# The order of a factorization kernel comes from 24 rounds of its list scheduler, with shorter transfer times in its model

## The chip, the cores and the metric

The kernel runs on one core of a Trainium2 chip. The metric is the device time of one execution in microseconds (us), as the median of several runs; less is better. The core has five instruction queues that run beside each other and meet through semaphores: TensorE (PE, matmuls into the PSUM banks), VectorE (DVE), ScalarE (ACT), GpSimd (POOL) and SyncE (SP, which only issues transfers). GpSimd issues transfers too. Each engine works through its own instructions strictly in the order in which the program was written, so an instruction whose input is late holds everything behind it on its engine.

## The reference

With x of 1024 x 512 and a weight of 64 x 512 x 512 (embedding e, feature f, model column m):

```python
out_lin = x @ lin_w.T + lin_b
xv = jnp.einsum('bf,efm->bem', x, weight)
zp = jnp.einsum('bf,efm->bem', jnp.square(x), jnp.square(weight))
interaction = 0.5 * jnp.sum(jnp.square(xv) - zp, axis=1)
return out_lin + interaction
```

So 64 products of 1024 x 512 by 512 x 512 are squared and summed over e. The second einsum needs only the sum over e of the squared weights, and so one product.

## The kernel before

The columns of the weight are worked off in groups of model columns: two narrow groups of 16 and twenty wide groups of 24, each with all 64 embeddings (`groups`, L41). In a group the product is not formed directly: x and the weight are each split in 2 x 2 blocks, and seven products of block sums replace eight (the loop over `ORDER` at L737, tiles X1 to X7 of x). Each of the seven is split again: six by the same scheme (`tree`, L513, seven products of two matmuls each), and product 1 in a wide group by a scheme of 20 smaller products (`wide_tree`, L598, HK at L20). What saves matmuls costs adds: block sums of the weight are made by GpSimd (the `t` tiles) and by transfers that add into memory (`dma_add`, L342), and the partial products that come out of PSUM are combined by VectorE, ScalarE and GpSimd into the tiles `oa`, `ob` and `c`. A finished block is squared by ScalarE (`square`, L324) and summed over e by VectorE (`reduce`, L328) into `acc`. The squares of the weight (`wsq`) go the same way into `w2_sum`.

PSUM is small: four pairs of banks, `b1`, `b3`, `b2_0` and `b2_1`. A product that accumulates into a bank can't start before VectorE or ScalarE has read what it held. So the reads of the banks (`tt`, L301, and `copy`, L315) release matmuls, and matmuls release reads.

None of this is emitted in the order of the source. Each helper records an operation in a `Plan` (L45) with a modelled duration for each engine that can do it, and with the operations that it depends on. A matmul has a `key`, its place in the intended sequence of TensorE. `Plan.order` (L76) then runs once: it gives every operation a latest start, worked back from the time at which the matmuls that need it would run if TensorE never waited, and plays the program through in modelled time. Whenever an engine is free, `pick` (L127) gives it the ready operation with the smallest latest start; TensorE takes the ready matmul of the smallest key within 20 us of its plan. The sequence in which operations were picked is the program, engine by engine. Only the order survives: the chip keeps no modelled time. Transfers have a modelled duration as well (`dma`, L339; `dma_add`, L342; the weight loads in `load`, L471), during which SyncE counts as taken.

After the last group an epilogue squares x once more (L775 to L783, which overwrites tiles that are free by then), adds the stored `acc` and linear parts (`add_acc`, L789) and multiplies by `w2_sum` (L805 to L826).

Of the kernel before, what the change touches and what calls it, by code (L numbers as in the profile page):

```python
# [32 lines left out]
HLEAD = 0  # L33
TBUF = 3
SPARE = -99.0
AHEAD = 20.0
APART = True
PE, DVE, ACT, POOL, SP = "PE", "DVE", "ACT", "POOL", "SP"
# [6 lines left out]
class Plan:  # L45
# [27 lines left out]
            op.key = op.after = max(key, op.after + 1e-6)  # L73
        self.ops.append(op)

    def order(self, spare=SPARE):  # L76
        ops = self.ops
        chain = sorted((o for o in ops if o.key is not None), key=lambda o: o.key)
        t = 0.0
        for o in chain:  # L80
            o.latest = t
            t += o.costs[PE]
        for o in reversed(ops):
            for d in o.deps:
                ops[d].succ.append(o.n)
            o.waits = [ops[d] for d in o.deps if o.key is None or ops[d].key is None]
        waiting = [len(o.succ) for o in ops]
        stack = [o for o in ops if not o.succ]
        while stack:
            o = stack.pop()  # L90
            latest = t if o.latest is None else o.latest
            cost = min(o.costs.values()) + o.land + self.HOP
            for x in o.succ:
                if o.key is None or ops[x].key is None:
                    latest = min(latest, ops[x].latest - cost)
            o.latest = latest
            for d in o.deps:
                waiting[d] -= 1
                if not waiting[d]:
                    stack.append(ops[d])  # L100
# [26 lines left out]
        def pick(e, now):  # L127
            if e == PE:
                able = [n for n in pending[e]
                        if ops[n].latest < now - late + AHEAD and ready(ops[n]) <= now + 1e-6]  # L130
                return ops[min(able, key=lambda n: ops[n].key)] if able else None
            if APART and e == POOL and free[DVE] > now + 0.1 and running[DVE].both:
                return None
            at = {n: ready(ops[n]) for n in pending[e]}
            for n in sorted((n for n in at if at[n] <= now + 1e-6),
                            key=lambda n: (ops[n].latest, n)):
                o = ops[n]
                if len(o.costs) > 1 and e == DVE and o.latest + late - now > spare:
                    continue
                if APART and o.both and e == DVE and free[POOL] > now + 0.1:  # L140
                    continue
                until = now + o.costs[e]
                if not any(
                    now + 1e-6 < at[u] < until - 0.2
                    and ops[u].latest < o.latest
                    and ops[u].latest + late < until + 0.1
                    for u in at
                ):
                    return o
            return None  # L150

        while len(done) < len(ops):
            now = heapq.heappop(times)
            moved = True
            while moved:
                moved = False
                for e in pending:
# [4 lines left out]
                        continue  # L162
                    moved = True
                    if e == PE:
                        late = max(late, now - o.latest)
                    cost = o.costs[e]

                    if e == DVE and o.both and free[POOL] > now + 0.1:
# [51 lines left out]
def kernel(  # L220
# [121 lines left out]
    def dma_add(o, i, rows, reads, writes):  # L342
        token = ("token", len(plan.ops))

        def emit(_):
            nc.gpsimd.dma_start(o, i, accum_op=ALU.add)

        cost = 2.9 * rows / 1024
        plan.add({POOL: 1.0}, emit, reads + writes, writes + (token,), land=cost + 2.5)
        plan.add({SP: cost}, None, (token,), ())  # L350

# [119 lines left out]
    def load(g, names):  # L471
        iw = GROUPS[g] // 2 * E
        for name, q in names:
            for k in range(KH):
                o = reg(name, k * iw, iw)
                dma(o.ap, source(g, q)[:, k * iw:(k + 1) * iw], (), o.atoms, 2.4 * iw / 1024)

    def outer_sum(g, which):
        o, i = {
# [404 lines left out]
```

## Time and profile before

| | us |
|---|---|
| median of 3 runs | 1427.72 |
| lowest and highest of them | 1426.12 and 1429.38 |
| span of the profiled execution, first to last instruction | 1425.4 |
| TensorE busy in it, matmuls | 1407.8 |
| VectorE busy | 1123.7 |
| ScalarE busy | 731.2 |
| GpSimd busy | 1093.3 |

The profiled execution has a span and no time of its own beside it; the runs that give the median were made without a profile. In the views below a row of instructions in order of time gives the start in us from the span's start, the duration, engine, line, operation, what is written from what (buffer numbers left out), shape and count, and in brackets the engine's idle time before it and what ended it. A product of the kernel is one matmul in the source and two matmul records in the trace. Rows of L356 are products of the two schemes, of L309 adds, of L335 sums over e, of L319 and L318 copies out of PSUM, of L779 and L793 the epilogue.

### The profile page before, as it was taken

To read this page: it belongs to the slowest core of one execution; us is meant where nothing else is said; L and a number is where in the kernel's file an instruction comes from. 1 tells how busy PE (TensorE), PEld (TensorE's weight loads), DVE (VectorE), ACT (ScalarE), POOL (GpSimd) and SP (SyncE) were. 2 spreads that over 40 slices of the span, in tenths; PEclk is the share of its full clock that TensorE was granted. 3 is DMA by queue.
4 is the path that set the end of the run, shared out by engine and by line. 5 is a ranking of instruction groups with operands and counts; after the bars stand their busy time and mean duration, and the time that the engine had idled before them with its cause. 6 is when DMAs were issued, how large, how long until landed. Compare 5 with 4: busy or idle time off the path is not lost.

```text
span 1425.4 us, 14830 instructions
## 1 busy us (share of the span) xinstructions
PE 1407.8 (99%) x4680; PEld 883.2 (62%) x4680; DVE 1123.7 (79%) x1365; ACT 731.2 (51%) x1048; POOL 1093.3 (77%) x895
## 2 busy tenths in 40 slices
PE   8999999999999999999999999999999999999998
PEld 3887565666656566665656566665656666565653
DVE  2678778796977879697887879687787969778875
ACT  2446545463645646464554646465464646455431
POOL 7897869696787869687776968787686968878670
PEclk9999999999999999999999999999999999999999
DMA  7667636464653646465463645555364646545241
GB/s 237 183 142 177 150 84 160 116 142 109 141 130 95 163 89 162 102 138 135 109 155 86 156 118 133 125 125 136 89 166 102 156 104 143 129 99 133 67 131 61
DMA packets 78893, 184.53 MB, mean 129 GB/s; under 512 B 28064, under 2 KB 29088, under 8 KB 78816
## 3 DMA queue, kind: packets, MB, share of 16 engines
q1 hardware_dynamic: 65488, 115.17, 27.5%
q0 software_dynamic: 12752, 67.38, 25.1%
q10 hardware_dynamic: 576, 1.05, 0.2%
q8 instruction: 38, 0.62, 0.2%
q14 instruction: 39, 0.32, 0.1%
HBM read 127.04 MB, written 6.19 MB: 93 GB/s over the span
## 4 chain that ended last, share of the span: by engine, by line
PE 91%; DVE 6%; issue 1%; DMA 1%; POOL 1%; ACT 0%; SPq 0%; DVEq 0%; POOLq 0%
PE b L356 75%; PE b_r L356 6%; PE b_l L356 6%; DVE acc L335 1%; DVE ob L309 1%; PE b_l L393 1%; DVE oa L309 1%; PE b_r L393 1%; PE b_l L813 1%; PE b_r L813 1%; DVE p L309 1%; DVE w_sum L335 1%; DMA X<-xT 1%; DVE c L309 0%; DMA ob<-lin_wT 0%
## 5 line engine op out<-in xcount | busy, mean ns | idle before, releaser
L356 PE MATMUL b<-t,X 128*128 128x384 f32 (+1 forms) x2144 | 720.9, 476 | 5.1 <-DVE oa L309 3.3
L356 PEld LDWEIGHTS b<-t,X 128*128 128x128 f32 x2144 | 403.2, 190 | 266.9 <-issue 23.2
L356 PE MATMUL b<-w,X 128*128 128x384 f32 (+1 forms) x816 | 276.1, 474 | 0.0
L309 POOL TENSOR_TENSOR t<-w 128x768 f32<-128x768 f32 (+1 forms) x128 | 182.4, 1431 | 119.7 <-PE b_l L356 104.4
L326 ACT ACTIVATE oa<-oa 128x768 f32<-128x768 f32 (+1 forms) x176 | 144.6, 824 | 201.6 <-DVE oa L309 182.9
L356 PEld LDWEIGHTS b<-w,X 128*128 128x128 f32 x816 | 154.6, 190 | 98.3 <-ACT p L319 13.0
L319 ACT COPY p<-b 128x768 f32<-128x768 f32 (+1 forms) x158 | 122.3, 774 | 173.4 <-PE b L356 173.2
L335 DVE TENSOR_REDUCE acc<-oa 128x12 f32<-128x768 f32 (+1 forms) x176 | 158.6, 921 | 39.9 <-ACT oa L326 39.8
L335 DVE TENSOR_REDUCE w_sum<-wsq 128x12 f32<-128x768 f32 (+1 forms) x176 | 158.6, 921 | 27.7 <-ACT wsq L326 27.7
L309 POOL TENSOR_TENSOR t<-w,t 128x384 f32<-128x384 f32 (+1 forms) x136 | 141.9, 1043 | 4.9
L319 ACT COPY b<-b 128x768 f32<-128x768 f32 (+1 forms) x134 | 102.5, 765 | 74.7 <-PE b L356 70.1
L309 DVE TENSOR_TENSOR oa<-b,oa 128x768 f32<-128x768 f32 (+1 forms) x66 | 61.3, 929 | 86.1 <-PE b L356 86.1
L326 ACT ACTIVATE wsq<-w 128x768 f32<-128x768 f32 (+1 forms) x132 | 104.9, 823 | 46.8 <-DMA w<-weight 31.8
L309 POOL TENSOR_TENSOR ob<-ob,p 128x768 f32<-128x768 f32 (+1 forms) x44 | 78.8, 1791 | 22.9 <-DVE p L309 22.9
L326 ACT ACTIVATE c<-c 128x768 f32<-128x768 f32 (+1 forms) x88 | 70.4, 819 | 47.9 <-DVE c L309 46.6
L356 PE MATMUL b<-T,X 128*128 128x384 f32 (+1 forms) x264 | 92.3, 476 | 0.0
L309 POOL TENSOR_TENSOR t<-t,w 128x256 f32<-128x256 f32 (+1 forms) x80 | 90.2, 1202 | 0.0
L309 DVE TENSOR_TENSOR ob<-b,oa 128x768 f32<-128x768 f32 (+1 forms) x66 | 61.3, 929 | 30.0 <-PE b L356 30.0
L309 DVE TENSOR_TENSOR p<-b,p 128x768 f32<-128x768 f32 (+1 forms) x88 | 81.5, 926 | 1.1 <-ACT wsq L326 0.6
L326 ACT ACTIVATE ob<-ob 128x768 f32<-128x768 f32 (+1 forms) x88 | 71.0, 826 | 21.6 <-DVE ob L309 14.6
L309 DVE TENSOR_TENSOR oa<-oa,b 128x768 f32<-128x768 f32 (+1 forms) x88 | 81.2, 923 | 0.8
L309 DVE TENSOR_TENSOR ob<-ob,b 128x768 f32<-128x768 f32 (+1 forms) x88 | 80.0, 926 | 2.0 <-PE b L356 1.4
(118 smaller groups left out, 2130.8 us busy)
## 6 DMA issues: line engine op xcount, KB each, us to landing
w<-weight SPq DMA_DIRECT2D x120, 384.0 KB, 3.5
T<-weight SPq DMA_DIRECT2D x40, 384.0 KB, 4.2
w<-T POOLq DMA_DIRECT2D x20, 768.0 KB, 5.8
T1a<-weight SPq DMA_DIRECT2D x20, 384.0 KB, 3.7
w22a<-weight SPq DMA_DIRECT2D x20, 384.0 KB, 3.2
T1a<-weight POOLq DMA_DIRECT2D x10, 768.0 KB, 7.9
T<-T1a POOLq DMA_DIRECT2D x10, 768.0 KB, 7.5
T1b<-weight SPq DMA_DIRECT2D x20, 384.0 KB, 4.5
```

Of the source, the lines that this page charges most:

```text
L309: return f(o.ap, a.ap, b.ap)
L319: return nc.scalar.copy(o.ap, i.ap)
L326: lambda _: nc.scalar.activation(o.ap, i.ap, AF.Square), i.atoms, o.atoms)
L335: nc.vector.tensor_reduce(o, x, axis=AX.X, op=ALU.add)
L356: nc.tensor.matmul(a.ap, b.ap, w.ap, start=start, stop=True, skip_group_check=True)
L393: nc.tensor.matmul(o[j].ap, x.ap[:, ts((g * 2 + j) % (NB // 2), P)], w.ap, start=(k == 0), stop=(k == NK - 1),)
L813: nc.tensor.matmul(z.ap, view(xe[h, k // KH])[:, k % KH, ts((g * 2 + j) % (NB // 2), P)], reg("w2_sum", k * M, M).ap, start=(k == 0), stop ...
```

## The change

`Plan.order` no longer plays the program through once. It calls the former body, now `schedule`, 24 times. After each round `blame` goes through the matmuls in the order of the round. For one that began more than 0.05 us later than TensorE was free, it follows back, up to 12 steps, what the matmul waited for: the slowest input of an operation if that came last, or else the operation before it on its engine. Each operation of that chain gets a `boost`, twice the time lost and at least 0.4 us, which makes its latest start earlier in the following rounds; boosts add up. The round in which the last matmul ends soonest in the model is the program. Matmuls keep their own due times (`due`), which boosts don't move. The modelled duration of a transfer that adds goes from 2.9 to 2.4 us per 1024 columns, and that of a weight load from 2.4 to 2.0.

```diff
+ROUNDS = 24
+CHAIN = 12
+PUSH = 2.0
...
-    def order(self, spare=SPARE):
+    def order(self):
+        boost, best = defaultdict(float), None
+        for o in reversed(self.ops):
+            for d in o.deps:
+                self.ops[d].succ.append(o.n)
+            o.waits = [self.ops[d] for d in o.deps
+                       if o.key is None or self.ops[d].key is None]
+        for _ in range(ROUNDS):
+            done = self.schedule(boost)
+            end = max(o.end for o, e in done if e == PE)
...
+            if best is None or end < best[0]:
+                best = end, done
+            self.blame(done, boost)
+        return best[1]
+
+    def blame(self, done, boost):
+
+        before, last, free = {}, {}, 0.0
+        for o, e in done:
+            before[o.n] = last.get(e)
+            last[e] = o
+            o.engine = e
+
+        def slowest(o):
+            return max((self.ops[d] for d in o.deps), key=lambda d: d.end, default=None)
+
+        for o, e in done:
+            if e != PE:
+                continue
+            lost = o.end - o.costs[PE] - free
+            free = o.end
+            if lost < 0.05:
+                continue
+            x = slowest(o)
+            for _ in range(CHAIN):
+                if x is None or x.engine == PE:
+                    break
+                begin = x.end - x.land - x.costs[x.engine]
+                y = slowest(x)
+                if y is not None and y.end + self.HOP > begin - 0.03:
+                    x = y
+                    continue
+                boost[x.n] += PUSH * max(lost, 0.2)
+                x, y = before[x.n], x
+                if x is None or x.latest > y.latest + 0.5:
+                    break
+
+    def schedule(self, boost, spare=SPARE):
         ops = self.ops
         chain = sorted((o for o in ops if o.key is not None), key=lambda o: o.key)
         t = 0.0
         for o in chain:
-            o.latest = t
+            o.latest = o.due = t
             t += o.costs[PE]
...
-            latest = t if o.latest is None else o.latest
+            latest = t if o.key is None else o.due
...
-            o.latest = latest
+            o.latest = latest - boost[o.n]
...
-                        if ops[n].latest < now - late + AHEAD and ready(ops[n]) <= now + 1e-6]
+                        if ops[n].due < now - late + AHEAD and ready(ops[n]) <= now + 1e-6]
...
-                        late = max(late, now - o.latest)
+                        late = max(late, now - o.due)
...
-        cost = 2.9 * rows / 1024
+        cost = 2.4 * rows / 1024
...
-                dma(o.ap, source(g, q)[:, k * iw:(k + 1) * iw], (), o.atoms, 2.4 * iw / 1024)
+                dma(o.ap, source(g, q)[:, k * iw:(k + 1) * iw], (), o.atoms, 2.0 * iw / 1024)
```

In the two built programs every engine has the same instructions, shape by shape. Their places differ for 170 of TensorE's 2340 products, 366 of VectorE's 1365 instructions, 354 of ScalarE's 1052, 326 of GpSimd's 895 and 13 of the 317 transfers that SyncE issues. Lines of the changed kernel are 49 higher from `Plan` on. Three places follow; the numbers at names are buffers, `b1`, `b3`, `b2_0` and `b2_1` the pairs of banks.

VectorE at the end of the fifth group (its last product, 3,), before and after the change:

```order
L335 TENSOR_REDUCE w2_sum_91<-wsq0_87 128x12
L335 TENSOR_REDUCE acc0_89<-oa_77 128x2x6
L335 TENSOR_REDUCE w2_sum_91<-wsq1_88 128x12
L309 TENSOR_TENSOR oa_77<-oa_77,b2_1 128x2x384
L309 TENSOR_TENSOR ob_78<-ob_78,b2_1 128x2x384
L309 TENSOR_TENSOR ob_78<-b2_0,ob_78 128x2x384
L335 TENSOR_REDUCE acc0_89<-oa_77 128x2x6
L309 TENSOR_TENSOR ob_78<-ob_78,b3 128x2x384
```

```order
L384 TENSOR_REDUCE w2_sum_91<-wsq0_87 128x12
L384 TENSOR_REDUCE w2_sum_91<-wsq1_88 128x12
L358 TENSOR_TENSOR ob_78<-b2_0,ob_78 128x2x384
L358 TENSOR_TENSOR ob_78<-ob_78,b3 128x2x384
L358 TENSOR_TENSOR oa_77<-oa_77,b2_1 128x2x384
L358 TENSOR_TENSOR ob_78<-ob_78,b2_1 128x2x384
L384 TENSOR_REDUCE acc0_89<-oa_77 128x2x6
```

The reads of `b2_0` and `b3` moved ahead of the two reads of `b2_1`, and one sum over e went from ahead of all four to behind them.

TensorE at the end of the second, narrow group (products 5 and 3 of the outer scheme, with tiles X5 and X3), before and after:

```order
L356 MATMUL b3<-t1_81,X3_64 128x256 x2
L356 MATMUL b2_0<-t0_80,X5_66 128x256 x2
L356 MATMUL b3<-w22b_73,X3_64 128x256 x2
L356 MATMUL b1<-w22b_73,X3_64 128x256 x2
L356 MATMUL b2_0<-t0_80,X5_66 128x256 x2
L356 MATMUL b2_1<-t1_81,X3_64 128x256 x2
L356 MATMUL b1<-w22b_73,X3_64 128x256 x2
L356 MATMUL b2_1<-t1_81,X3_64 128x256 x2
L356 MATMUL b3_r<-t2_82,X1_62 128x256
```

```order
L405 MATMUL b3<-t1_81,X3_64 128x256 x2
L405 MATMUL b1<-w22b_73,X3_64 128x256 x2
L405 MATMUL b2_0<-t0_80,X5_66 128x256 x2
L405 MATMUL b3<-w22b_73,X3_64 128x256 x2
L405 MATMUL b2_1<-t1_81,X3_64 128x256 x2
L405 MATMUL b2_0<-t0_80,X5_66 128x256 x2
L405 MATMUL b1<-w22b_73,X3_64 128x256 x2
L405 MATMUL b2_1<-t1_81,X3_64 128x256 x2
L405 MATMUL b3_r<-t2_82,X1_62 128x256
```

The first product into `b1` moved ahead by two pairs, and the first into `b2_1` by one.

VectorE in the last group, where the first squares of the epilogue (`SCALAR_TENSOR_TENSOR` on the tiles `w11` and `X1`) stand among the reads of product 6, before and after:

```order
L309 TENSOR_TENSOR ob_78<-b2_0,oa_77 128x2x384
L779 SCALAR_TENSOR_TENSOR w11_69<-w11_69 128x1024
L309 TENSOR_TENSOR ob_78<-ob_78,b3 128x2x384
L309 TENSOR_TENSOR ob_78<-b1,oa_77 128x2x384
L309 TENSOR_TENSOR ob_78<-b2_0,p5_0_83 128x2x384
L779 SCALAR_TENSOR_TENSOR X1_62<-X1_62 128x1024
```

```order
L358 TENSOR_TENSOR ob_78<-b2_0,oa_77 128x2x384
L358 TENSOR_TENSOR ob_78<-ob_78,b3 128x2x384
L358 TENSOR_TENSOR ob_78<-b1,oa_77 128x2x384
L358 TENSOR_TENSOR ob_78<-b2_0,p5_0_83 128x2x384
L828 SCALAR_TENSOR_TENSOR w11_69<-w11_69 128x1024
L828 SCALAR_TENSOR_TENSOR X1_62<-X1_62 128x1024
```

The square of `w11` moved behind three reads of the banks.

More of the change, by code (lines that the diff above doesn't have):

```diff
@@ L35 @@
 SPARE = -99.0
+ROUNDS = 24
+CHAIN = 12
+PUSH = 2.0
+TALK = False
 AHEAD = 20.0
@@ L74, in add @@
         self.ops.append(op)
-    def order(self, spare=SPARE):
+    def order(self):
[8 more added lines that the diff above has]
+            end = max(o.end for o, e in done if e == PE)
+            if TALK:
+                print(_, round(end, 2))
+            if best is None or end < best[0]:
[31 more added lines that the diff above has]
+    def schedule(self, boost, spare=SPARE):
         ops = self.ops
```

4 lines of the change are left out of this document (removed).

## The prediction

> **What bounds the kernel now.** I read the page's busy times and its chain first, then the waits of TensorE, then stages, then single instructions in order of time.
>
> ```profile
> PE 1407.8 (99%) x4680; PEld 883.2 (62%) x4680; DVE 1123.7 (79%) x1365; ACT 731.2 (51%) x1048; POOL 1093.3 (77%) x895
> ...
> PE 91%; DVE 6%; issue 1%; DMA 1%; POOL 1%; ACT 0%; SPq 0%; DVEq 0%; POOLq 0%
> ```
>
> TensorE is busy for 1407.8 of the 1425.4 us of the span, and the change takes no matmul away. So the prize is small: what TensorE loses between matmuls. Of the 17.6 us of idle time, the longest single wait lies at the start, before the first weights land, and no order of the queues moves it:
>
> ```profile
> PE b_l L393 <- DMA ob<-lin_wT: 6.1, 1, 6.1
> PE b L356 <- DVE oa L309: 3.3, 3, 2.8
> ```
>
> Idle time is not the whole loss, since a matmul that starts late behind a pipelined one shows as busy. I therefore count from start to start. This view of TensorE by stages gives elapsed time, busy time and matmul records (two per product):
>
> ```profile
> 36.30:126.87 90.57, 89.76 (x401) 1.00 0.65 171
> 441.46:504.42 62.96, 62.96 (x209) 1.00 0.54 127
> 1337.05:1390.64 53.59, 48.72 (x149) 1.00 0.44 128
> ```
>
> The first row is the two narrow column groups, the second one of the 20 wide groups in its steady run (no idle time: nothing to win there), the third the last group. The granted clock (the 1.00) is full in all three. So what the change can win lies in the narrow groups, in a few wide groups that do not run like the second row, and in the last one.
>
> **The change part by part.** Every engine keeps its instructions, shape by shape; the rounds and the shorter transfer times in the planner's model only reorder them. Nothing is removed or added on the chip, so each term is a wait of TensorE that goes, and a step that was ahead and is late instead.
>
> *The end of the fifth group.* TensorE's rows (start, duration, count) and then VectorE's at the same place:
>
> ```profile
> 307.57 2.74 PE L356 MATMUL b<-t,X 128*128 128x384 f32 x8
> 310.15 1.45 PE L356 MATMUL b<-w22a,X 128*128 128x384 f32 x4
> 311.89 1.56 PE L356 MATMUL b<-t,X 128*128 128x384 f32 x4 [0.28 <-DVE ob L309]
> 313.61 0.70 PE L356 MATMUL b_r<-t,X 128*128 128x256 f32 x2 [0.16 <-DVE ob L309]
> 314.14 1.03 PE L356 MATMUL b_l<-t,X 128*128 128x256 f32 x4
> ```
>
> ```profile
> 307.44 0.94 DVE L335 TENSOR_REDUCE acc<-oa 128x12 f32<-128x768 f32 x1
> 308.29 0.95 DVE L335 TENSOR_REDUCE w_sum<-wsq 128x12 f32<-128x768 f32 x1
> 309.15 0.95 DVE L309 TENSOR_TENSOR oa<-oa,b 128x768 f32<-128x768 f32 x1
> 310.01 0.95 DVE L309 TENSOR_TENSOR ob<-ob,b 128x768 f32<-128x768 f32 x1
> 310.88 0.95 DVE L309 TENSOR_TENSOR ob<-b,ob 128x768 f32<-128x768 f32 x1
> 311.75 0.95 DVE L335 TENSOR_REDUCE acc<-oa 128x12 f32<-128x768 f32 x1
> 312.60 0.95 DVE L309 TENSOR_TENSOR ob<-ob,b 128x768 f32<-128x768 f32 x1
> ```
>
> Eight matmuls of 384 columns take 2.58 us from start to start (307.57 to 310.15), so four take 1.29. From 310.15 to 311.89 are 1.74 us, 0.45 lost; to 313.61 another 1.72, 0.43 lost; the next two of 256 columns take 0.53 to 314.14, where a later paragraph shows 0.43, 0.10 lost: **0.98 us** in all. TensorE waits here for the reads at 310.88 and 312.60, which empty the banks that it must write. The new order puts both directly behind the reduce at 308.29, and TensorE makes the product that the first of them reads one pair earlier. That pair then ends where the pair at 307.57 has its first half, near 309.0; the two reads end near 310.0 and 310.9, and TensorE wants the banks at 311.4 and 312.7. Both waits go. Late instead by two slots (1.7 us) are the adds of 309.15 and 310.01, whose bank is next written after the products at 313.61, so that is covered by about one slot. I take 0.9.
>
> *The end of the sixteenth group* has the same pair of waits:
>
> ```profile
> 1004.97 1.45 PE L356 MATMUL b<-w22b,X 128*128 128x384 f32 x4
> 1006.71 1.56 PE L356 MATMUL b<-t,X 128*128 128x384 f32 x4 [0.29 <-DVE ob L309]
> 1008.43 0.70 PE L356 MATMUL b_r<-t,X 128*128 128x256 f32 x2 [0.16 <-DVE ob L309]
> ```
>
> By the same count 0.45 and 0.43. Here the new order moves only the first read ahead of an add; the second still stands behind three adds that cannot begin before their products. I take the first alone, 0.45, with bounds 0 and 0.98.
>
> *The narrow groups.* At the end of the second one TensorE's starts are uneven:
>
> ```profile
> 118.18 1.97 PE L356 MATMUL b<-w22b,X 128*128 128x256 f32 x8
> 119.99 2.02 PE L356 MATMUL b<-t,X 128*128 128x256 f32 x8
> 121.84 1.03 PE L356 MATMUL b<-w22b,X 128*128 128x256 f32 x4
> 123.00 1.13 PE L356 MATMUL b<-t,X 128*128 128x256 f32 x4
> 124.19 0.70 PE L356 MATMUL b_r<-t,X 128*128 128x256 f32 x2
> 124.72 1.03 PE L356 MATMUL b_l<-t,X 128*128 128x256 f32 x4
> 125.58 1.03 PE L356 MATMUL b<-t,X 128*128 128x256 f32 x4
> ```
>
> Four matmuls of 256 columns take 0.86 us (124.72 to 125.58). From 118.18 the steps are 1.81, 1.85, 1.16, 1.19 and 0.53 where 1.72, 1.72, 0.86, 0.86 and 0.43 would do: 0.09, 0.13, 0.30, 0.33 and 0.10, **0.95 us**. The new order on TensorE sets the products into `b1` and `b2_1` one pair earlier, and VectorE's reads of `b2_1` and `b3` stand ahead of four reduces. I take 0.9. In the whole window of 90.57 us, 401 records at 0.215 would take 86.2, so 4.4 are lost and 3.4 remain. Some of those waits lose a reduce or a GpSimd add from ahead of them, others keep their rows and their order: the bounds are 0 and 3.4, and I take 0.8, about a quarter, since the order on TensorE is nearly unchanged there.
>
> *The last group.* A square of the input for the epilogue stands on VectorE between two reads that TensorE waits for:
>
> ```profile
> 1339.63 1.54 PE L356 MATMUL b<-t,X 128*128 128x384 f32 x4
> 1341.74 1.53 PE L356 MATMUL b<-t,X 128*128 128x384 f32 x4 [0.57 <-DVE ob L309]
> ```
>
> ```profile
> 1339.51 1.23 DVE L779 SCALAR_TENSOR_TENSOR w<-w 128x1024 f32<-128x1024 f32 x1
> 1340.65 0.95 DVE L309 TENSOR_TENSOR ob<-ob,b 128x768 f32<-128x768 f32 x1
> ...
> 1347.25 0.96 DVE L309 TENSOR_TENSOR oa<-b,oa 128x768 f32<-128x768 f32 x1 [2.79 <-PE b L356]
> ```
>
> From 1339.63 to 1341.74 are 2.11 us, 0.82 over the 1.29. The new order moves the 1.23 us of the square behind three reads; it then lies in the 2.79 us that VectorE idles before 1347.25, and if that cover were gone it would cost its 1.23. I take 0.8.
>
> *The steady groups.* Their matmuls keep their order, or nearly so, and reductions, squares and GpSimd's adds change places beside them. The second window has no idle time to win, and I value this at 0, as the wide groups' engines other than TensorE have slack (79% at most). Thirteen of the transfers that SyncE issues move, nearly all in the first two groups, a weight load going ahead of stores that wait for VectorE; its first reader stands a whole group later, so it costs nothing while the earlier loads keep their cover.
>
> *What stays.* The largest wait of the last group is a transfer's, with VectorE's queue held behind it in the same order as before:
>
> ```profile
> 1361.53 1.56 PE L356 MATMUL b<-t,X 128*128 128x384 f32 x4 [2.78 <-DVE oa L309]
> ```
>
> **Sum:** 0.9 + 0.45 + 0.9 + 0.8 + 0.8 = 3.85 us. Each is on TensorE's path, and no later wait but that last transfer's could swallow it; that transfer is issued when TensorE has done with the tile that it overwrites, and so moves along. The profiled span of 1425.4 becomes 1421.5. What lies around the span is taken as the 2.3 us between it and the median of 1427.72; the profiled execution has no other time. **Forecast: 1423.9 us**, 0.27% faster.
>
> **The rivals.**
>
> *The waits move one product on.* Where a read goes ahead of an add, TensorE may wait for that add. For it: the sixteenth group's second wait, which I already leave in. Against: the fifth group, where TensorE's order changes too. If only the last group's 0.8 and half of the two ends (0.45 + 0.45) hold, 1.7 is won: 1426.0. Much the same would come if the change does not do what it says, because what delays a matmul in the planner's model is not what delays it here.
>
> *More of the narrow groups.* If all of the 3.4 went rather than 0.8: 1421.3.
>
> *The tail's add is not held.* Both rows start at one instant, VectorE's and GpSimd's:
>
> ```profile
> 1385.16 2.84 DVE L793 SCALAR_TENSOR_TENSOR T1b<-w,T1b 128x976 f32<-128x976 f32 x1
> 1385.16 1.80 POOL L309 TENSOR_TENSOR ob<-ob,p 128x768 f32<-128x768 f32 x1
> ```
>
> 2.84 is GpSimd's 1.80 and 1.04 more, as if VectorE had stood still until GpSimd was done. What starts first is decided by some ns. If VectorE does, it is 1.80 sooner there, TensorE's last products follow at most by that, and the time is 1422.1. Both queues keep their order here, so it is not likely. [...]
>
> *Slower: the filler is missed.* In four groups, the seventh among them, two products that have all their inputs stand before the wide ones, and the new order sets them 13 places later. A ScalarE copy feeds the last of the wide ones:
>
> ```profile
> 382.23 1.47 PE L356 MATMUL b<-T,X 128*128 128x384 f32 x4
> ...
> 385.26 1.89 PE L356 MATMUL b_r<-w,X 128*128 128x256 f32 x8
> ```
>
> ```profile
> 382.70 0.59 ACT L318 ACTIVATE b_r<-b_r 128x512 f32<-128x512 f32 x1
> ```
>
> Without the filler's 1.29 the products of 385.26 come to 383.97, and the copy ends at 383.29: 0.68 us to spare. From a copy later by more than that, TensorE stands, for up to 1.29 us a group: 5.2 in four groups. With the 3.85 won elsewhere that is 1.35 slower, 1429.1; if the ends win nothing either, 1432.9. Against it: the new order also sets VectorE's step ahead of that copy sooner.
>
> **How the numbers follow.** Forecast 0.55, with a range of its own from 1422.2 to 1425.0. Waits that move on 0.22 (1426.0). All of the narrow groups 0.06 (1421.3). The add not held 0.07 (1422.1). The missed filler 0.10 (1429.1, in a third of it 1432.9). A measurement of this kernel can tell about 0.2%, 2.9 us. Faster by more than that are nine tenths of the forecast's cases, the narrow groups and the add, 0.62 rounded; slower by more than that a part of the last, 0.04; the rest, 0.34, is within. The range from 1421.2 to 1427.6 leaves out most of the slow case and a little of the fast ones, under 2 in 10.
>
> **What would show it.** In the profile after: no wait of TensorE for VectorE's `ob` at the ends of the fifth group and the second, one of two left at the sixteenth's; the square behind the three reads and TensorE's starts 1.29 apart around 1340; the 2.8 us wait in the last group still there; matmul records of the steady groups spaced as before. The prediction is wrong if TensorE's total idle time falls by less than 1 us, if new waits stand ahead of the wide products, or if the steady groups need more than 62.96 us each.

## The result and the profile after

| | before | after |
|---|---|---|
| median, us | 1427.65 (1426.12 to 1429.38, 4 runs) | 1421.52 (1421.01 to 1424.34, 4 runs) |
| ratio | | 0.9962, 95% interval 0.9948 to 0.9976 |
| span of the profiled execution, us | 1425.4 | 1419.6 |

A second comparison gave 1421.89 us (5 runs) against 1426.96 (14 runs), ratio 0.9965, interval 0.9952 to 0.9978. The change makes the kernel 0.2 to 0.5% faster. 1423.9 was forecast, so the gain is some 5 to 6 us where 3.85 was the sum.

The page of the changed kernel, busy times and chain:

```profile
PE 1405.6 (99%) x4680; PEld 885.2 (62%) x4680; DVE 1122.6 (79%) x1365; ACT 741.5 (52%) x1048; POOL 1094.6 (77%) x895
...
PE 95%; DVE 2%; DMA 1%; POOL 1%; issue 0%; ACT 0%; SPq 0%; DVEq 0%; ACTq 0%; POOLq 0%
```

TensorE's waits after, with their sum, their count and the longest:

```profile
PE b_l L442 <- DMA ob<-lin_wT: 6.3, 1, 6.3
PE b L405 <- DVE oa L358: 2.3, 3, 1.6
```

The same stages as before, elapsed time, busy time and matmul records, then the granted clock:

```profile
441.46:504.42 62.96, 62.96 (x210) 1.00 0.53 127
1337.05:1390.64 53.59, 51.73 (x157) 1.00 0.40 114
```

The engines do the same work; TensorE's share of the chain rises from 91 to 95%. The steady group is what it was. In the last group's 53.59 us TensorE idles 1.86 where it idled 4.87, and the longest wait for VectorE falls from 2.8 to 1.6 us. So part of the gain is where the prediction looked; how much must be taken stage by stage.

For that I list every matmul that starts later than its forerunner's start plus that one's time in an undisturbed run (0.216, 0.322 and 0.428 us for 256, 384 and 512 columns), if by over 0.025 us, and add up by stage. Each kernel was profiled twice. The last column is the term of the prediction.

| stage, us from the span's start | before | before, second | after | after, second | forecast gain |
|---|---|---|---|---|---|
| to 13, first products | 2.74 | 1.82 | 1.97 | 1.83 | 0 |
| 13 to 126.5, narrow groups | 4.24 | 5.96 | 3.81 | 3.83 | 1.7 |
| to 290 | 0.40 | 0.40 | 0.98 | 0.96 | 0 |
| to 320, end of the fifth group | 1.01 | 1.01 | 0.06 | 0.06 | 0.9 |
| to 980 | 2.84 | 2.83 | 2.67 | 2.64 | 0 |
| to 1020, end of the sixteenth | 1.02 | 1.01 | 0.54 | 0.54 | 0.45 |
| to 1330 | 0.66 | 0.64 | 0.75 | 0.73 | 0 |
| to 1350, square of `w11` | 0.90 | 0.85 | 0.08 | 0.08 | 0.8 |
| to 1370, transfer from `xT` | 3.55 | 3.78 | 2.37 | 2.36 | 0 |
| to the end, add into `T1b` | 1.52 | 0 | 0 | 0 | 0 |
| sum | 18.87 | 18.31 | 13.23 | 13.05 | 3.85 |

The first pair differs by 5.64. With the first product 0.17 us later (6.11, then 6.27) and 0.36 less from the last product to the span's end, that is the 5.8 of the spans. Every engine's order is the same in the two profiles of one kernel, so a difference between them is chance: 0.9 in the first products (the first records of 512 columns are 0.85 us apart instead of 0.43, and in before there are more of them), 1.7 in the narrow groups of before, 1.5 at the add.

**What went as forecast.** TensorE and VectorE at the end of the fifth group after the change (start, duration, shape, count):

```profile
309.66 1.46 PE L405 MATMUL b<-w22a,X 128*128 128x384 f32 x4
310.95 1.46 PE L405 MATMUL b<-t,X 128*128 128x384 f32 x4
312.24 0.60 PE L405 MATMUL b_r<-t,X 128*128 128x256 f32 x2
```

```profile
308.67 0.96 DVE L358 TENSOR_TENSOR ob<-b,ob 128x768 f32<-128x768 f32 x1 [0.41 <-ACT oa L375]
309.66 0.95 DVE L358 TENSOR_TENSOR ob<-ob,b 128x768 f32<-128x768 f32 x1
```

Starts are 1.29 us apart and no idle time stands in brackets. The two reads end at 309.6 and 310.6, and TensorE comes to their banks at 310.95 and 312.24. At the sixteenth group one of two waits is left, the one that was forecast:

```profile
1006.41 0.70 PE L405 MATMUL b_r<-t,X 128*128 128x256 f32 x2 [0.17 <-DVE ob L358]
```

In the last group, TensorE, then VectorE with the moved squares and the GpSimd add beside them:

```profile
1337.70 2.83 PE L405 MATMUL b<-t,X 128*128 128x384 f32 x8
1340.37 2.75 PE L405 MATMUL b<-w,X 128*128 128x384 f32 x8
```

```profile
1339.40 0.95 DVE L358 TENSOR_TENSOR ob<-b,p 128x768 f32<-128x768 f32 x1
1340.27 1.22 DVE L828 SCALAR_TENSOR_TENSOR w<-w 128x1024 f32<-128x1024 f32 x1
1341.40 2.83 DVE L828 SCALAR_TENSOR_TENSOR X<-X 128x1024 f32<-128x1024 f32 x1
1344.51 0.96 DVE L358 TENSOR_TENSOR oa<-b,oa 128x768 f32<-128x768 f32 x1 [0.28 <-PE b L405]
```

```profile
1340.49 2.65 POOL L358 TENSOR_TENSOR ob<-ob,oa 128x768 f32<-128x768 f32 x1 [2.89 <-DVE ob L358]
```

From 1337.70 eight records of 384 columns take 2.67 us, nearly the undisturbed 2.58. The second square now runs beside a GpSimd add and takes 2.83 us where it took 1.22; VectorE's idle time behind it, 2.79 before, is 0.28. The cover that the prediction named was nearly used up.

**What did not.** New waits in the narrow groups (the first for a ScalarE copy, the second for VectorE's read):

```profile
71.80 1.99 PE L405 MATMUL b<-t,X 128*128 128x256 f32 x8 [0.46 <-ACT p L368]
...
117.10 1.13 PE L405 MATMUL b<-w22b,X 128*128 128x256 f32 x4 [0.43 <-DVE oa L358]
118.07 1.03 PE L405 MATMUL b<-t,X 128*128 128x256 f32 x4
118.93 1.03 PE L405 MATMUL b<-w22b,X 128*128 128x256 f32 x4
```

From 118.07 on the starts are 0.86 us apart, as forecast for the end of the second group, but a wait of 0.43 stands ahead of them. Two more new waits stand ahead of products of the 20-product scheme, at 187.27 and 250.53 us, 0.36 us each from start to start (0.06 at the same products before). There VectorE's read into `oa` now comes behind both reads into `ob`, and the ScalarE copy ahead of those products waits for it until 186.65 and 249.91 us. New waits ahead of wide products were one of the prediction's signs of being wrong; they came at a small size. And the wait for the transfer, which was to stay at its size, is shorter:

```profile
1357.61 1.56 PE L405 MATMUL b<-t,X 128*128 128x384 f32 x4 [1.60 <-DVE oa L358]
```

### The profile page after: what moved, and what is told of

It is laid out like the page before. It is cut to its first block, busy times and chain, and to the rows that moved or that the text cites. A ratio compares the mean times of both kernels' runs of the same rounds, so it can differ in the third digit from the quotient of the medians.

```text
span 1419.6 us, 14838 instructions
## 1 busy us (share of the span) xinstructions
PE 1405.6 (99%) x4680; PEld 885.2 (62%) x4680; DVE 1122.6 (79%) x1365; ACT 741.5 (52%) x1048; POOL 1094.6 (77%) x895
## 4 chain that ended last, share of the span: by engine, by line
PE 95%; DVE 2%; DMA 1%; POOL 1%; issue 0%; ACT 0%; SPq 0%; DVEq 0%; ACTq 0%; POOLq 0%
PE b L405 79%; PE b_r L405 6%; PE b_l L405 6%; PE b_l L442 1%; PE b_r L442 1%; PE b_r L862 1%; PE b_l L862 1%; DVE ob L358 1%; DVE oa L358 1%; DMA X<-xT 0%; POOL oa L358 0%; DMA w<-weight 0%; DMA ob<-lin_wT 0%; POOL ob L358 0%; DVE acc L384 0%
## 5 line engine op out<-in xcount | busy, mean ns | idle before, releaser
L358 POOL TENSOR_TENSOR t<-w 128x768 f32<-128x768 f32 (+2 forms) x128 | 179.1, 1400 | 107.5 <-PE b_l L405 97.5
L358 POOL TENSOR_TENSOR t<-t,w 128x256 f32<-128x256 f32 (+1 forms) x80 | 96.4, 1208 | 3.2 <-PE b L405 3.0
```

Of the source, the lines that this page charges most:

```text
L358: return f(o.ap, a.ap, b.ap)
```

## Experiments

Theories. *Order*: each wait is made or removed by the instructions that stand around it, as the prediction took it. *Carried over*: a stretch's waits depend on what lies before it (buffers, transfers under way). *Chance*: some of the difference comes with executions, not with the order. For the transfer's wait a fourth: an *instruction fetch* that falls on the same DMA engines.

Each ratio is taken against runs of before that were made beside the kernel; it is not the quotient of two medians of this table.

| kernel | median, us | ratio to before, 95% interval |
|---|---|---|
| e1, before again | 1427.06, one run | |
| e2, after again | 1421.89 | 0.9965 (0.9952 to 0.9978) |
| e3, 24 rounds, former transfer times | 1424.20 | 0.9986 (0.9977 to 0.9996) |
| e4, new transfer times, one round | 1440.99 | 1.0096 (1.0079 to 1.0113) |
| e5, narrow groups alone | 1424.93 | 0.9985 (0.9975 to 0.9994) |
| e6, the two ends alone | 1425.57 | 0.9988 (0.9979 to 0.9997) |
| e7, square of `w11` alone | 1425.33 | 0.9990 (0.9982 to 0.9999) |
| e8, late square moved, on before | 1423.20 | 0.9971 (0.9959 to 0.9982) |
| e9, narrow groups, later joint | 1423.68 | 0.9979 (0.9970 to 0.9988) |
| e10, late square moved, on after | 1420.38 | 0.9954 (0.9941 to 0.9966) |
| e11, best stretches | 1420.04 | 0.9956 (0.9942 to 0.9970) |
| e12, after with 55 small matmuls | 1445.20, one run | |

### The two halves of the change: e1 to e4

e1 and e2 are the two kernels themselves.

> The kernel before, unchanged, for a second profile. Three pieces of the 5.8 us between the two profiled spans have rows that no order decides: VectorE's add into T1b took 2.84 us before and 1.16 after (it and a GpSimd add start within 0.01 us of each other in both), the transfer into X took 8.0 and 6.9 us, the slow first matmuls cost 2.7 and 2.0 us. Theory 'chance': they vary from execution to execution of one program; here at least one of them comes out near the value of after, and the span falls by that (1422.5 to 1425). Theory 'order': the program sets them; all three are within 0.2 us of the first profile, span 1425.4 within 0.7.

> The changed kernel, unchanged, for a second profile and an interval. Theory 'order': span 1419.6 within 0.7, the T1b add 1.16, PE's last wait 1.76 lost at the X transfer; ratio 0.996. Theory 'chance': the T1b add is held again (2.8) or the X transfer takes 8 us in this execution, span 1421 to 1423.

```diff
 # e3: the rounds, with the former transfer times
-        cost = 2.4 * rows / 1024
+        cost = 2.9 * rows / 1024
-... 2.0 * iw / 1024)
+... 2.4 * iw / 1024)
 # e4: the new transfer times, one round
-ROUNDS = 24
+ROUNDS = 1
```

> 24 rounds with the transfer times of before in the model. Theory 'rounds': the pushes for late matmuls make the gain, so this has nearly all of it, ratio 0.995 to 0.9975 and the waits at the ends of the fifth and sixteenth group gone. Rival 'transfer times': without the shorter transfers the rounds start from the order of before, gain little, ratio 0.998 to 1.000.

> One round, that is no pushes, with the shorter transfer times. Theory 'rounds': no gain from the order, 0.999 to 1.001, and the 0.45 and 0.43 us waits for reads of banks still at the ends of some wide groups. Rival 'transfer times': the order that weight loads and adding transfers get moves most of the gain, 0.9955 to 0.998.

The shorter transfer times alone make the kernel 1% slower, which neither theory expected: e4 loses 32.6 us in the sum of the table above, 13.8 more than before, and not at one place (7.8 in the narrow groups, 9.3 between 320 and 980 us). Up to 3.4 us of it come from two drops of TensorE's clock, each 3.41 us at half (last section). The rounds win that back and more. Rounds alone give 0.9986, where the rival for e3 had 0.998 to 1.000, and both give 0.9965. So the shorter times are no gain in themselves, and the rounds need them for most of theirs. Why the rounds end at a better order with them is not shown.

e2 came out as *order* says (span 1419.5 us, the add 1.16, the transfer's loss 1.76). Before again shows what chance does. Its first narrow products and its tail's add:

```profile
36.81 1.10 PE L356 MATMUL b<-t,X 128*128 128x256 f32 x4 [0.86 <-DVE c L309]
...
40.34 1.10 PE L356 MATMUL b<-t,X 128*128 128x256 f32 x4 [0.62 <-ACT b L319]
```

```profile
1386.52 2.85 POOL L309 TENSOR_TENSOR ob<-ob,p 128x768 f32<-128x768 f32 x1
1386.53 1.16 DVE L793 SCALAR_TENSOR_TENSOR T1b<-w,T1b 128x976 f32<-128x976 f32 x1
```

The two waits at 36.81 and 40.34 are not in the first profile. The add that took 2.84 us there takes 1.16 here, and now GpSimd's takes 2.85 instead of 1.80; nothing in the program differs. The span is 1425.3 us all the same, because the narrow groups lose 1.7 us more. Of the seven profiles that have the order of before at this place, one has the long add.

### One stretch at a time: e5, e6, e7, e9

These kernels keep the order of before and take a stretch of every queue from the order of the changed kernel. Both orders are made in the kernel; a stretch is cut where, on each engine, the instructions ahead of the cut are the same ones in both.

```diff
 # e5
+PARTS = [(0.0, 128.0)]
 # e6
+PARTS = [(290.0, 320.0), (980.0, 1020.0)]
 # e9
+PARTS = [(0.0, 140.0)]
...
+        seq = {e: list(a[e]) for e in a}
+        for lo, hi in PARTS:
+            lo, hi = cut(lo), cut(hi)
+            for e in a:
+                seq[e][lo[e]:hi[e]] = b[e][lo[e]:hi[e]]
```

The numbers are modelled times, some 6 us below the trace's. e7 moves one instruction in the finished order of before, three places down VectorE's queue:

```diff
-    for op, engine in plan.order():
+    done = plan.order()
+    later(("sq", 0, 0), 3)
+    for op, engine in done:
```

> The order of before everywhere except in the two narrow groups (to about 126 us), which have the order of the changed kernel; same instructions. In the profile of before TensorE loses 4.22 us from start to start between 13 and 126 us. Prediction: the end of the second group gives 0.9 and the rest 0.8, so 1.7 less, 2.5 lost there. Rival, waits that trade places: the moved instructions put waits of 0.63 at 71.80 us (for ScalarE's copy into p) and of 0.60 at 117.10 us (for VectorE's oa), as the profile of the changed kernel has them, so 3.8 lost there and only 0.4 us less than before. Every other stage as in before: 1.0 at the end of the fifth group, 0.9 at the square, about 3.5 at the transfer.

> As e5_narrow_part, but the joint between the two orders lies later (near 146 us instead of near 120), so that the end of the second narrow group has the order of the changed kernel too. In e5 TensorE lost 1.01 us at 123.67, just behind the joint, where before loses 0.33 and the changed kernel nothing. If that wait belonged to the joint, the loss between 13 and 126 us is 3.8 as in the changed kernel, against 4.2 to 6.0 in the profiles of the order of before (five of them); the prediction said 2.5. If the narrow groups of the new order depend on what the later groups do, it stays near 5.

The joint of e5 came out at some 120 us, ahead of the second group's last products, not at 126. Just behind it stands a new wait:

```profile
123.67 1.13 PE L478 MATMUL b<-t,X 128*128 128x256 f32 x4 [0.84 <-DVE ob L429]
```

So e5 lost 5.35 us in the narrow groups. With the later joint, e9 loses 3.83, the changed kernel's own 3.81 and 3.83. The order decides, and the rival of e5's text has it: the moved instructions remove waits and put others at 71.8 and 117 us. The gain is 0.4 against the first profile of before and 2.1 against the second. Five profiles with the order of before at this place (before twice, e6, e7, e8) lose 4.24, 5.96, 6.02, 4.24 and 5.03, mean 5.1; four with the new order 3.81, 3.83, 3.83 (e9) and 3.71 (e10), mean 3.8. On the mean the narrow groups bring 1.3 us.

> The order of before except at the ends of the fifth group (about 290 to 320 us) and of the sixteenth (about 980 to 1020 us), which have the order of the changed kernel. If each wait is made and unmade by the order around it, the loss goes from 1.01 to about 0.06 at the fifth and from 1.01 to 0.53 at the sixteenth, 1.4 us in all (prediction 0.9 + 0.45), and nothing else moves. Rival: the two gains come from what the earlier groups left behind (buffers that come free sooner, transfers that land sooner); then less than half of it, under 0.7 us.

TensorE in e6 at the joint ahead of the fifth group's end, and at the joint behind it:

```profile
295.09 1.24 PE L478 MATMUL b<-t,X 128*128 128x384 f32 x3 [0.75 <-DVE c L429]
```

```profile
313.25 1.45 PE L478 MATMUL b<-t,X 128*128 128x384 f32 x4
314.54 0.59 PE L478 MATMUL b_r<-t,X 128*128 128x256 f32 x2
...
320.20 1.24 PE L478 MATMUL b<-T,X 128*128 128x384 f32 x3 [0.26 <-DVE ob L429]
```

The two waits of the fifth group's end are gone, the sixteenth group loses 0.58 instead of 1.02, so the order at the place makes these waits. But the fifth's gain was paid back at the joints: the loss between 290 and 320 us is 1.08, as before, and 0.5 more lies behind 320.2. What this run shows is the mechanism, not the sum of 1.4 us. The ratios of e5, e6 and e9 hold 1.2 us more that their stretches have no part in: in all three the wait for the last transfer is the short one (next part).

> Before with one instruction moved: the square of w11 behind three reads of the banks on VectorE, as in the changed kernel. Theory that the order of this one instruction holds TensorE: the loss near 1341 us falls from 0.89 to about 0.1, 0.8 us, and nothing else moves but with it. Second question, the wait at the input's second transfer (2.94 us of loss in before, 1.76 in the changed kernel): if the moved square is what shortened it (VectorE reaches the wait in another state), it falls to about 1.8 here as well, 2.0 us in all; if the instruction fetch that lies on one of the DMA engines during the transfer made it long, and is still there, it stays near 3.

The loss at the square falls from 0.90 to 0.08; that term stands. The transfer's wait did not fall with it (next part), and the profile shows something more behind that wait. TensorE, and then its stages, with the granted clock behind the count in brackets:

```profile
1360.09 4.71 PE L356 MATMUL b<-t,X 128*128 128x384 f32 x8 [2.93 <-DVE oa L309]
```

```profile
1360.00:1362.00 2.00, 1.81 (x5) 0.84 0.98 376
1362.00:1365.20 3.20, 3.20 (x6) 0.57 0.06 21
1365.20:1368.00 2.80, 2.80 (x10) 1.00 0.00 0
```

In the trace's own record of the clock it is at half for 3.41 us, from 1361.36 us on. Eight matmuls take 4.50 us from start to start instead of 2.58, of which some 0.5 is lost behind this wait in the other profiles too. That is why this profile loses 5.12 in the transfer's stage, where before loses 3.55.

### The wait for the last transfer: e8, e12

The square of the input's last tile waits on VectorE for the transfer `X<-xT`; the reads that free TensorE's banks stand behind it. This transfer landed 8.0 us after its issue in before and 7.0 in after. The queues in that time (packets, MB, share of the 16 DMA engines) and the transfer, before:

```profile
q0 software_dynamic: 144, 0.79, 59.5%
q1 hardware_dynamic: 272, 0.52, 17.7%
q8 instruction: 1, 0.02, 1.4%
...
X<-xT SPq DMA_DIRECT2D x1, 512.0 KB, 8.0
```

and after, with the next transfer of the same size:

```profile
q0 software_dynamic: 144, 0.79, 68.1%
q1 hardware_dynamic: 282, 0.54, 23.0%
...
X<-xT SPq DMA_DIRECT2D x1, 512.0 KB, 7.0
T<-xT SPq DMA_DIRECT2D x1, 512.0 KB, 3.9
```

q0 is GpSimd's adding transfer, issued 1 us ahead; beside it a transfer takes 7.0 us, and one of the same size behind it 3.9. That the adding transfer makes the difference is not tested. q8 is the fetch of instructions, a 16 KB packet, 38 in a run. In before one falls into the transfer, from 1350.36 to 1352.21 us. TensorE runs 9360 matmuls and weight loads, 246 for each of the 38; that the packets are TensorE's own is my estimate from these two counts, and no run shows it. TensorE had no idle time while this packet moved. Of the profiles below, those with such a packet in the transfer's first 5.3 us have the longer transfer:

| profile | fetch starts after the transfer's issue by, us | transfer to the square, us | TensorE's loss, us |
|---|---|---|---|
| before | 0.6 | 8.0 | 2.9 |
| e1 | 1.6 | 8.3 | 3.2 |
| e7 | 0.6 | 8.2 | 3.1 |
| e4 | 5.3 | 8.5 | 3.2 |
| after, e2, e3 | ahead of it by 2.7 to 6.2 | 7.0 | 1.8 |
| e5, e6, e9 | ahead of it by 7.0 | 7.0 | 1.8 |

e5, e6 and e9 have the order of before in the whole tail, and the short wait. So these 1.2 us of the gain did not come from the order in the last group; the fetch is the difference that the traces show. Not every fetch inside the transfer counts: in e11 one starts 6.4 us behind the issue, and the transfer lands at 7.1 us; the next one of its size takes 4.6 us instead of 3.6 to 3.9.

The long stop has a second price, which neither profile of before shows. For each execution the mean granted clock is on record. Profiles that read 0.999 or 1.000 have no drop between the first product and the last, e7's reads 0.998 and has one, e4's 0.997 and has two. Of the executions of before that ran beside e1 to e11, 41 of 57 read 0.998 or less; of the changed kernel's none of 9, and of e5's and e6's, with the tail of before but the short wait, none of 22. So most executions of before probably have a drop like e7's. No profile shows where it lies, and four executions of e3 and e9 read as low without a long stop in their profiles. Beside e1 to e4, before took 1426.13 us where the clock read 1.000 (5 runs) and 1427.28 where it read 0.998 (9 runs); in the two later comparisons the difference is 0.7 and 0.2.

e12 moves the fetch:

```diff
+                n = 55 if k == g == 0 else 0
                 return [
+                    nc.tensor.matmul(o[0].ap[:, :64], x.ap[:, :P], w.ap[:, :64], start=True,
+                                     stop=True, skip_group_check=True)
+                    for _ in range(n)
+                ] + [
```

> The changed kernel with 55 small matmuls of 64 columns put ahead of the first product; they write into a bank that the first product overwrites, so only TensorE's count of instructions changes (220 more matmuls and weight loads, some 33 us of its 1412 at 9360 in all). Theory that the wait for the last transfer from xT is longer where an instruction fetch lies on one of the 16 DMA engines during that transfer: the fetches (38 in a run, one in about 37 us) come some 33 us earlier in the program, so the one at 1382 us in the changed kernel comes near 1349, inside the transfer (1347 to 1354 us, all of it moved by the few us that the small matmuls take); then X lands about 8 us after its issue instead of 6.9, VectorE idles 4.3 to 4.5 us ahead of the square instead of 3.3, and TensorE loses about 3.0 us there instead of 1.76. If the fetch is inside and the loss stays at 1.76, the fetch isn't the cause. If the fetch lies elsewhere (its moment varies by some 7 us between programs), the run tells nothing. The start is later by 2 to 7 us for the small matmuls.

The kernel is 23.5 us longer by the small matmuls, where 2 to 7 were expected. The fetch came 0.6 us after the transfer's issue. The transfer, VectorE's square and TensorE:

```profile
q8 instruction: 1, 0.02, 1.3%
...
X<-xT SPq DMA_DIRECT2D x1, 512.0 KB, 7.5
```

```profile
1377.61 2.00 DVE L833 SCALAR_TENSOR_TENSOR X<-X 128x1024 f32<-128x1024 f32 x1 [3.80 <-DMA X<-xT]
```

```profile
1381.39 1.56 PE L405 MATMUL b<-t,X 128*128 128x384 f32 x4 [2.34 <-DVE oa L358]
```

The direction is right and the size is not: 0.5 us of landing and 0.7 of TensorE's loss (2.50 against 1.76) where 1.0 and 1.2 were expected. The fetch lengthens the wait; how much depends on something that these runs don't show, and what sets a fetch's moment stays open as well.

e8 takes the wait out of TensorE's way, with one move on the order of before: `later(("sq", 1, 1), 6)`.

> Before with one other instruction moved: the square of the tile that the late transfer fills (X from xT, issued at 1349.75 us) goes behind the next six instructions of VectorE's queue, so that the reads that TensorE waits for no longer stand behind a wait for that transfer. Theory that TensorE waits for the transfer only through VectorE's queue: the loss at 1361.53 us of 2.94 (3.18 in the second look at before) and most of the 0.52 behind it go, 2.8 to 3.4 us, and the time is near 1424. Rival, the reads themselves are late (for GpSimd's sums or for TensorE's own products): less than 1 us is won. Slower would be the epilogue, if the squares now come too late for TensorE's last product.

All 3.55 us of the stage went, but 1.6 came back at the next reads. VectorE's two squares, then TensorE:

```profile
1362.29 2.68 DVE L779 SCALAR_TENSOR_TENSOR X<-X 128x1024 f32<-128x1024 f32 x1
1364.89 2.82 DVE L779 SCALAR_TENSOR_TENSOR T<-T 128x1024 f32<-128x1024 f32 x1
```

```profile
1370.48 0.91 PE L356 MATMUL b<-t,X 128*128 128x384 f32 x2 [1.38 <-DVE c L309]
```

Both squares run beside GpSimd's adds and take over twice their 1.21 us. VectorE's queue, not the data, tied TensorE to the transfer. Beside the adds the squares took 2.68 and 2.82 us, so the place to which the square goes should be free on GpSimd too.

### A better version: e10, e11

```diff
 # e10, on the changed kernel
+    later(("sq", 1, 1), 14)
+    later(("add", 2, 0), 6)
 # e11: the same moves; stretches by modelled time, 3 is the order of e3, 2 the changed kernel, before elsewhere
+PARTS = [(0.0, 140.0, 3), (284.5, 1e9, 2)]
```

> The changed kernel with two instructions of VectorE's queue moved back in the last stretch: the square of the tile that the late transfer fills goes behind 14 others (into VectorE's idle time near 1370 us, where GpSimd is idle too), and the epilogue's add into T1b goes behind 6. If VectorE's queue is all that ties TensorE to that transfer, the loss of 2.37 us between 1350 and 1370 us goes and the span falls from 1419.5 to about 1417.3, the ratio to before near 0.995. Rival, the wait moves on as it did in e8 (there 3.5 went and 1.6 came back at 1370 us, where two squares ran beside GpSimd's adds and took 2.7 and 2.8 us): under 1 us is won over the changed kernel.

TensorE in e10 where the wait was, and the square in its new place:

```profile
1354.67 3.71 PE L405 MATMUL b<-t,X 128*128 128x384 f32 x11
1358.22 2.74 PE L405 MATMUL b<-w,X 128*128 128x384 f32 x8
1360.80 1.45 PE L405 MATMUL b<-t,X 128*128 128x384 f32 x4
```

```profile
1367.66 1.21 DVE L828 SCALAR_TENSOR_TENSOR X<-X 128x1024 f32<-128x1024 f32 x1
```

The wait is gone (0.06 us lost in that stage, 2.37 in the changed kernel), 0.77 came back behind it, the span is 1417.9. Its 1420.38 us are 1.5 below the 1421.89 of the changed kernel, each against before in its own comparison; the intervals of the two ratios overlap.

> Put together from the order that loses least in each stretch, on the same instructions: the narrow groups in the order that the 24 rounds give with the former transfer times (e3: 2.5 us lost there, the changed kernel 3.8), the third to fifth group's begin in the order of before (0.38 lost, the changed kernel 0.95), the rest in the order of the changed kernel, and the two moves of e10. If the losses of the stretches add up, 1.3 + 0.6 + 2.3 = 4.2 us less than the changed kernel, a span near 1415.3. Rival: what comes before a stretch decides its waits (buffers, transfers under way), the joints make new ones (e3 lost 1.7 at 158 us, behind its narrow groups), and it is within 1.5 us of the changed kernel.

The losses do not add up. TensorE in the third group, which has the order of before here:

```profile
157.09 1.56 PE L487 MATMUL b<-t,X 128*128 128x384 f32 x4 [0.98 <-DVE oa L438]
```

The narrow groups lose 2.51 as in e3, and the third group pays e3's price for it (2.14 lost between 126.5 and 290 us, 0.40 in before), although its own order is that of before. e3 has a wait at this place too (1.28 us from start to start at 158.06), and e9, with the same joint behind another narrow order, has none. So here the wait is carried over. The result, 1420.04 us, is that of e10.

## Why the prediction was right, and where its sizes were off

The time fell into the stated range, near its lower end, and the mechanism held in the four stages that had a term. That it came out below the forecast, and still within the range, is partly luck: in the first profiles the gains that were not forecast (3.0 us) were larger than what the terms missed (1.2).

- **What bounds it.** Right: no engine's work changed, the gain is in TensorE's waits (and probably in its clock behind one of them), and the steady group is the same to 0.01 us.
- **End of the fifth group, 0.9.** Measured 0.95.
- **End of the sixteenth, 0.45.** Measured 0.48; the second wait stays, as forecast.
- **The square, 0.8.** Measured 0.82 and 0.77; alone, in e7, 0.8. Of its cover, 2.79 us of idle time, the second square beside GpSimd used nearly all.
- **Narrow groups, 0.9 + 0.8: mis-sized.** 0.43 and 2.13 in the two pairs of profiles, 1.3 on the mean. The end of the second group became even, as forecast, but the step overlooked that the reads that moved ahead put others behind (waits of 0.62 at 71.8 us and 0.60 at 117.1 us, counted from start to start). What came on top are waits at 36.8 and 40.3 us that the first profile of before happened not to have; none of the profiles with the new order has them.
- **Steady groups, 0: nearly.** Their waits changed by +0.57 between 126.5 and 290 us (the ends of the third and fourth groups), -0.18 to 980 and +0.09 to 1330. The rival of the missed filler did not come. The two new waits of 0.36 are of the other rival's kind: a read went ahead of an add, and a ScalarE copy, with TensorE behind it, now waits for that add.
- **"What stays", 0: the term that was mis-sized most.** The prediction took the wait's 2.8 us for the transfer's own, moving along with it. It fell by 1.2, and the runs put this down to an instruction fetch that fell into the transfer in before. I had not looked at what else moved on the DMA engines then.
- **The add into `T1b`.** I gave the free add a small chance because the order there is unchanged. The premise was wrong: one execution does not settle which of two instructions that start within 20 ns is held. The add is free in six of seven profiles of the old order, so its 1.5 us in the first pair of profiles is no gain of the change.

In the first profiles, the four stages with a term gave 2.7 of the 3.85, and things without a term 3.0 (1.2 transfer, 1.5 add, 0.8 first products, less 0.5 in the steady groups). With means in place of the first profiles, the change is worth about 0.95 + 0.48 + 0.8 + 1.3 + 1.2 - 0.5 = 4.2 us, of which the 1.2 probably hang on the fetch (e12, which moves it, gives 0.7 of them). The two measured ratios (3 to 7 us by their intervals) agree with that. What the profiles leave out is the drop of the clock: beside e1 to e4 the changed kernel is 4.2 us below the executions of before at a clock of 1.000, and 5.1 below all of them. So up to 0.8 us of the measured gain probably hang on the clock (0.2 and 0.6 by the two later comparisons), and on the same long stop.

The forecast took 2.3 us for what lies around the span. Where a time and a span of one execution are on record they differ by 1.8 (1421.4 and 1419.6 in the changed kernel, 1427.06 and 1425.3 in e1).

## What to carry to other kernels

A single profile does not price waits of a microsecond: profile the kernel before twice, and take only what both show. When a wait goes, ask of the queue that moved which reads now stand behind, and when an instruction waits for a transfer, look at everything on the DMA engines and at what is queued behind it. Waits in a list-scheduled program are made locally but also carried over, so pieces of two good orders need not make a better one.

## What was unexpected of the hardware

- A transfer with an instruction fetch of 16 KB inside it landed 0.5 to 1.4 us later (7.0 us otherwise), in five profiles (before, e1, e4, e7, e12); in before the one packet took 1.85 us. A fetch 6.4 us behind the issue (e11) left it at 7.1.
- TensorE's clock dropped to half behind stops of some 3 us (2.93 in e7, 3.1 the longest in e4). The traces record drops from 1361.36 us in e7 and from 106.00 and 1375.76 us in e4, each 3.41 us at half the full clock. The full clock from its first record to the drop after the last matmul lasts 1413.118 us in before and 1409.704 in the changed kernel, 414 and 413 steps of 3.4133 us. I divide each trace into such steps from the first record of its clock: each of the three drops begins at the end of a step, and in that step TensorE idled for 0.63, 0.63 and 0.90 of the time. In the twelve profiles without a drop no step was idle for more than 0.54 (before 0.54, e1 0.53, the changed kernel 0.47). So in these profiles it is not the stop alone that decides (2.93 us in e7 with a drop, 3.02 in e1 without) but, as far as three drops show it, how it lies to the steps. If a stop of 2.9 us falls evenly on the steps, and 0.6 of a step is enough, two thirds of the executions have a drop (an estimate from these numbers); 41 of 57 read a low clock. A stop of 1.6 us, as in the changed kernel, fills 0.47 of a step at most.
- A square on VectorE beside a GpSimd add took 2.68 to 2.83 us instead of 1.21, in the changed kernel, e7, e8 and e10. It can also be the add that is longer: at 1360.94 us in the changed kernel the square began 0.15 us ahead of an add and took its 1.21, and the add took 2.72 instead of some 1.8. Which of the two is held does not follow the recorded starts at the add into `T1b`: in all seven profiles of the old order GpSimd's row starts first, by 2 to 20 ns, and only at 2 ns was VectorE held.
